# First pair of row blocks by halves with eight products a step, chunks loaded ahead of x, and operands of x built two blocks at a time

## The chip, the core and the metric

The kernel runs on one core of a Trainium2 chip. The metric is the device time of one execution in microseconds (us); less is better. Engines: TensorE (PE, with its weight loads as PEld), VectorE (DVE), ScalarE (ACT), GpSimd (POOL), and SyncE (SP), which here only issues loads. Each engine takes its instructions in the order of the program.

## What is computed

Everything is float32; N is 4096 rows, D is 512 columns, `adj` is 4096 x 4096.

```python
def reference(x, adj, L1_gnn_W):
    # layer 0
    mask = adj > 0
    head = mask / max(sqrt(sum(mask * mask, axis=-1)), 1e-12)
    inc = adj + head
    y = (inc @ x) / sum(inc, axis=-1)
    x = layernorm(x + y)
    # layer 1
    A2 = adj + eye
    dscale = diagonal(A2) ** -0.5
    temp = A2 @ x @ W.T
    x = layernorm(x + relu((dscale[:, None] * A2 * dscale[None, :]) @ temp))
    return x
```

(This is the reference in short; names are shortened.)

## The kernel before

Rows and columns of the large matrices are halved, and a product of 2 x 2 blocks is made of seven products of sums of blocks (S1 to S4 from the left operand, T1 to T4 from the right one) instead of eight. Layer 0 is the part that the change touches. It works on 16 *pairs* j: row blocks j and j + 16 of 128 rows each. The inner dimension of a pair is 16 *steps* kk (blocks kk and kk + 16 of x), taken in four *chunks* of four steps. One chunk of `adj` is a tile `a` of 128 partitions x 4 quarters x 512 (1 MB), with the quarters in the order A12, A11, A22, A21: the first two belong to the upper row block, the last two to the lower. A step is seven products with a 128 x 128 left operand and 256 columns (258 with the ones column that gives the row sums), accumulated in seven PSUM banks over the 16 steps (`multiply1`, L417).

The order of the work is written by hand: the program order is the order on every engine. Around a chunk it is: load the chunk after next (`load_chunk`, on SP's queue), prepare the next chunk (`prepare1`, on DVE), multiply this one (`multiply1`), count signs for a later pair (`count`, on ACT).

`prepare1` per chunk: raw sums A11 + A21 and A22 + A21 for layer 1 (L383), stored by POOL's queue (`oa`, L403); for each half the mask (`adj > 0`) times the row's scale (L393) and its addition to `a` (L395); then S1 to S4 (`add_up`, L159 to L162). On the main diagonal the identity goes into the raw sums (L166).

The scale of a row is one over the root of its number of positive entries. Since the rows lie on the free axis of a chunk, the scale has to stand in every partition. For pairs 1 to 15, ACT counts signs in tiles of `adj` in its natural layout (`nat`, 128 x 512, five buffers, loaded on SP's queue, L302 and L336), 16 tiles a pair; `spread` then sums, takes the root and the reciprocal, puts it on a diagonal `d`, and a product with ones spreads it over the partitions (L368), copied to `sc` (L370). For pair 0 it is counted from the chunks themselves (`count_first`): ACT makes bfloat16 signs of each whole chunk, 32 products with ones sum them up (L320), and DVE and ACT take root and reciprocal of 256 values (L306 to L323). This needs all four chunks of pair 0, so the fourth is loaded into an extra tile (`last`), and once more later as a chunk.

A block of x has a slot `b` of seven operands: B11, B21, B22 (raw quarters of x), T1, T2, T3 and T4; the fourth raw quarter, B12, is loaded in the place of T4. `build` makes T1 to T4 with four DVE operations of 128 x 256 (L123 to L126). The slots stay for the whole of layer 0.

At the start SP's queue holds: x of steps 0 to 3 (two loads of 256 KB each, L289 and L290), three chunks and `last` (1 MB each), then x of steps 4 to 15 with five `nat` loads among them. DVE builds the first four slots, then waits for the scale, prepares chunk 0 in four pieces of one step each, and in pair 0 builds the four slots of the next chunk ahead of each `prepare1` (L494 to L496). At the end of a pair, `combine` puts the seven banks together into the upper and lower row block; `layer0` normalises them and `operands` stores them for layer 1 in the course of the next pair.

Of the kernel before, what the change touches and what calls it, by code (L numbers as in the profile page):

```python
# [8 lines left out]
F32 = mybir.dt.float32  # L9
# [17 lines left out]
def tile_adj_resnorm_d2(  # L27
# [79 lines left out]
    nc.gpsimd.memset(tiny, -(2.0 ** -63))  # L107
    dscale = const.tile([P, NB], F32, name="dscale")
# [12 lines left out]
    def outer_sums(t, b11, b12, b21, b22):  # L121

        nc.vector.tensor_sub(t[:, 0, :], b11, b12)  # L123
        nc.vector.tensor_sub(t[:, 2, :], b22, b12)
        nc.vector.scalar_tensor_tensor(t[:, 1, :], t[:, 0, :], -1.0, b22, op0=ALU.mult, op1=ALU.subtract)
        nc.vector.tensor_add(t[:, 3, :], b21, t[:, 1, :])  # L126
# [142 lines left out]

    ones_f = w1_pool.tile([P, P], F32, name="ones_f", bufs=1)  # L270
    nc.gpsimd.memset(ones_f, 1.0)
    ones_b = w1_pool.tile([P, P], BF16, name="ones_b", bufs=1)
    nc.gpsimd.memset(ones_b, 1.0)
# [3 lines left out]
    def half_tile(dtype=F32, width=CW):  # L277
        return w1_pool.tile([P, 2, width], dtype, tag="u", name="u", bufs=3)
# [6 lines left out]
    def load_x(kk):  # L285

        s = feats_pool.tile([P, 7, W], F32, name=f"b{kk}")
        lo, hi = x[kk * P:(kk + 1) * P, :], x[(kk + NP) * P:(kk + NP + 1) * P, :]
        nc.sync.dma_start(out=s[:, B11:T4 + 1:T4, 0:H], in_=split(lo))  # L289
        nc.sync.dma_start(out=s[:, B21:B22 + 1, 0:H], in_=split(hi))  # L290
        nc.gpsimd.memset(s[:, B11:B21 + 1, H:W], 1.0)
        nc.gpsimd.memset(s[:, T1, H:W], 1.0)
        slots[kk] = s

    def build(kk):

        s = slots[kk]
        outer_sums(s[:, T1:T4 + 1, 0:H], s[:, B11, 0:H], s[:, T4, 0:H], s[:, B21, 0:H], s[:, B22, 0:H])
# [5 lines left out]
    def to_scale(n, total):  # L304

        nc.vector.tensor_scalar(n, total, 0.5, N / 2, op0=ALU.mult, op1=ALU.add)  # L306
        nc.vector.tensor_scalar(n, n, EPS * EPS, None, op0=ALU.max)
        nc.scalar.activation(n, n, AF.Sqrt)

    def count_first(parts):  # L310

        ps = spare()[:, 0:2 * P].rearrange("p (h i) -> p h i", h=2)
        for c, a in enumerate(parts):
            m = half_tile(BF16, 2 * CW)
            m = m.rearrange("p h (q i) -> p (h q) i", q=2)
            signs(m, a)
            for i in range(CK):
                for z in range(2):
                    first, last = c + i + z == 0, c == NC - 1 and i == CK - 1 and z == 1
                    nc.tensor.matmul(ps, ones_b, m[:, z::2, i * P:(i + 1) * P], start=first, stop=last)  # L320
        s = w1_pool.tile([P, 2, P], F32, name="sc")
        to_scale(s, ps)
        nc.vector.reciprocal(s, s)  # L323
        scale[0] = s
# [24 lines left out]
    spreading = {}  # L349

    def spread(j, part):

        if part == 0:
# [3 lines left out]
            spreading[j] = n  # L357
        elif part == 1:
            n = spreading.pop(j)
            nc.vector.reciprocal(n, n)  # L360
            d = w1_pool.tile([P, 2, P], F32, name="d", bufs=1)
            for h in range(2):
                nc.vector.tensor_scalar(d[:, h, :], ident, n[:, h:h + 1], None, op0=ALU.mult)
            spreading[j] = d
        else:
            d = spreading.pop(j)
            ps = spare()
            nc.tensor.matmul(ps[:, 0:2 * P], ones_f, d.rearrange("p h i -> p (h i)"), start=True, stop=True)  # L368
            s = w1_pool.tile([P, 2, P], F32, name="sc")
            nc.scalar.copy(s.rearrange("p h i -> p (h i)"), ps[:, 0:2 * P])  # L370
            scale[j] = s

    def prepare1(n, pieces=1):


        j, c = divmod(n, NC)
        a, s = chunks[n], scale[j]
        sr, *masks = (half_tile() for _ in range(3))
        sums[n] = work.tile([P, 4, CW], F32, tag="s", name="s")
        for i in range(pieces):  # L380
            w = CW // pieces
            cols = slice(i * w, (i + 1) * w)
            nc.vector.tensor_add(sr[:, :, cols], a[:, A11:A22 + 1, cols],  # L383
                                 a[:, A21, cols].unsqueeze(1).to_broadcast([P, 2, w]))
            for h in range(2):
                t = masks[h]
                y, z = t[:, :, cols], a[:, 2 * h:2 * h + 2, cols]
                if pieces == 1:
                    parts = [[v.rearrange("p q (b i) -> p (q b) i", i=P) for v in (y, z)]]
                else:  # L390
                    parts = [[v[:, q, :].rearrange("p (b i) -> p b i", i=P) for v in (y, z)] for q in range(2)]
                for m, v in parts:
                    nc.vector.scalar_tensor_tensor(m, v, 0.0, s[:, h, :].unsqueeze(1).to_broadcast(list(v.shape)),  # L393
                                                   op0=ALU.is_gt, op1=ALU.mult)
                nc.vector.tensor_add(a[:, 2 * h:2 * h + 2, cols], a[:, 2 * h:2 * h + 2, cols], t[:, :, cols])  # L395
            add_up(sums[n][:, :, cols], a[:, :, cols])
# [8 lines left out]
    def multiply1(n, acc):  # L405
        c = n % NC
        a, s = chunks.pop(n), sums.pop(n)
        for i in range(CK):
            kk = c * CK + i
            b = slots[kk]  # L410
            cols = slice(i * P, (i + 1) * P)
            for m, (left, right, w) in enumerate((
# [4 lines left out]
                nc.tensor.matmul(acc[m][:, 0:w], left, b[:, right, 0:w], start=(kk == 0), stop=(kk == NP - 1))  # L417

# [49 lines left out]
    for kk in range(CK):  # L468
        load_x(kk)
    for n in range(3):  # L470
        load_chunk(n)
    last = work.tile([P, 4, CW], F32, tag="s", name="s")
    nc.sync.dma_start(out=last, in_=adj_q[0, NC - 1])
    for kk in range(CK, NP):
        load_x(kk)
        if kk >= 2 * CK and len(waiting) < 5:
            load_natural()
    for kk in range(CK):
        build(kk)
    count_first([chunks[0], chunks[1], chunks[2], last])  # L480
    prepare1(0, pieces=CK)

    C = None
    for n in range(NP * NC):
        j, c = divmod(n, NC)
        if c == 0:
            if j > 0:
                C = combine(acc)
            acc = [bank(m) for m in range(7)]
        if n + 2 >= NP * NC:  # L490
            load_up_to(n + 2 - NP * NC)
        elif n > 0:
            load_chunk(n + 2)
        if j == 0 and c < NC - 1:  # L494
            for kk in range((c + 1) * CK, (c + 2) * CK):
                build(kk)  # L496
        if j + 1 < NP and c == (3 if j == 0 else 2):
            spread(j + 1, 0)
            if j == 0:
                spread(1, 1)  # L500
                spread(1, 2)
        if n + 1 < NP * NC:
            prepare1(n + 1)
        else:
            prepare(0)
        if 0 < j < NP - 1 and c == 2:
            spread(j + 1, 1)
        multiply1(n, acc)
        if 0 < j < NP - 1 and c == 2:
            spread(j + 1, 2)  # L510
        count(((5, 5, 6, 4) if j == 0 else (6, 6, 0, 4))[c])
# [4 lines left out]
        if j > 0 and c == 1:  # L516
            layer0(j - 1, C)
        if j > 0 and c == 2:
# [294 lines left out]
```

## Time and profile before

| | us |
|---|---|
| median of 3 runs | 2346.43 (2346.09 to 2346.45) |
| the profiled execution | 2345.41 |
| its span, first to last instruction | 2343.6 |
| TensorE busy in the span | 2277.4 (97%) |
| DVE busy | 1832.7 (78%) |
| ACT busy | 351.5 (15%) |
| mean granted TensorE clock | 0.990 of full |

All durations come from the profiled execution, which lasted 1.0 us less than the median of the runs. "Busy" is the time in which an engine worked on an instruction; weight loads are counted apart and lie beside the products. Line numbers (L417) are lines of the kernel before. In the chain of waits each piece is the work that held up what follows it; the page leaves out pieces too short to matter. An arrow such as `a<-adj_q` says which tile was written from which tensor. A float32 product on TensorE leaves two records in the trace.

### The profile page before, as it was taken

To read this page: it belongs to the slowest core of one execution; us is meant where nothing else is said; L and a number is where in the kernel's file an instruction comes from. 1 tells how busy PE (TensorE), PEld (TensorE's weight loads), DVE (VectorE), ACT (ScalarE), POOL (GpSimd) and SP (SyncE) were. 2 spreads that over 40 slices of the span, in tenths; PEclk is the share of its full clock that TensorE was granted. 3 is DMA by queue.
4 is the path that set the end of the run, shared out by engine and by line. 5 is a ranking of instruction groups with operands and counts; after the bars stand their busy time and mean duration, and the time that the engine had idled before them with its cause. 6 is when DMAs were issued, how large, how long until landed. Compare 5 with 4: busy or idle time off the path is not lost.

```text
span 2343.6 us, 21028 instructions
## 1 busy us (share of the span) xinstructions
PE 2277.4 (97%) x7166; PEld 1352.6 (58%) x7166; DVE 1832.7 (78%) x2727; ACT 351.5 (15%) x806; POOL 220.7 (9%) x372
## 2 busy tenths in 40 slices
PE   4999999999999999999999999999999999999996
PEld 3788888888888844444444444444444444444443
DVE  6898888888889857888666779766567798767796
ACT  3232333323333000000000000000000011200013
POOL 0011111111111110000001100011100000000010
PEclk8999999999999999999999999999999999999998
DMA  9577777777776466575566757567666576765672
GB/s 318 197 252 252 262 244 253 258 255 260 251 256 235 172 261 242 207 276 204 202 252 229 274 186 267 186 237 286 225 238 223 214 253 237 267 231 216 224 260 77
DMA packets 148011, 552.97 MB, mean 236 GB/s; under 512 B 15920, under 2 KB 24128, under 8 KB 108864
## 3 DMA queue, kind: packets, MB, share of 16 engines
q1 hardware_dynamic: 114192, 418.42, 51.0%
q0 software_dynamic: 33712, 133.21, 14.9%
q8 instruction: 57, 0.93, 0.2%
q14 instruction: 50, 0.41, 0.0%
HBM read 438.32 MB, written 113.25 MB: 235 GB/s over the span
## 4 chain that ended last, share of the span: by engine, by line
PE 86%; DVE 8%; issue 3%; DMA 2%; ACT 0%; POOL 0%; SPq 0%; ACTq 0%; DVEq 0%; POOLq 0%
PE q L252 55%; PE q L417 26%; PE q L625 5%; DVE a L395 1%; DVE u L393 1%; DVE s L159 1%; DMA a<-oa 1%; DVE u L383 1%; DMA s<-adj_q 1%; DVE s L161 1%; PE q L645 1%; DMA oa<-u 0%; DVE c L553 0%; DVE s L162 0%; PE q L368 0%
## 5 line engine op out<-in xcount | busy, mean ns | idle before, releaser
L252 PE MATMUL q<-s,ts 128*128 128x512 f32 x1344 | 616.0, 594 | 1.0 <-DVE u L544 1.0
L417 PE MATMUL q<-b,s 128*128 128x256 f32 (+1 forms) x2048 | 488.5, 381 | 2.3 <-DVE s L161 2.3
L159 DVE TENSOR_TENSOR s<-a 128x1024 f32<-128x1024 f32 (+1 forms) x243 | 294.1, 1210 | 203.5 <-PE q L252 173.8
L252 PEld LDWEIGHTS q<-s,ts 128*128 128x128 f32 x1344 | 256.2, 191 | 325.7 <-issue 296.6
L417 PEld LDWEIGHTS q<-b,s 128*128 128x128 f32 x2048 | 389.8, 190 | 61.0 <-DVE s L161 3.7
L417 PE MATMUL q<-b,a 128*128 128x258 f32 (+1 forms) x1536 | 381.8, 383 | 10.1 <-issue 10.1
L252 PE MATMUL q<-a,tr 128*128 128x512 f32 x704 | 333.5, 596 | 5.1 <-DMA tr<-ob 4.2
L417 PEld LDWEIGHTS q<-b,a 128*128 128x128 f32 x1536 | 293.9, 192 | 52.9 <-issue 10.7
L252 PE MATMUL q<-s,tr 128*128 128x512 f32 x448 | 228.8, 592 | 0.0
L252 PEld LDWEIGHTS q<-a,tr 128*128 128x128 f32 x704 | 132.1, 191 | 162.1 <-issue 158.1
L302 ACT ACTIVATE nat<-nat,tiny 128x512 f32<-128x512 f32 x240 | 171.0, 715 | 208.2 <-DMA nat<-adj 208.1
L252 PE MATMUL q<-a,ts 128*128 128x512 f32 x352 | 180.2, 593 | 3.1 <-DVE c L549 2.9
L393 DVE SCALAR_TENSOR_TENSOR u<-a,sc 128x1024 f32<-128x1024 f32 (+1 forms) x142 | 157.6, 1114 | 24.8 <-ACT sc L370 14.4
L161 DVE TENSOR_TENSOR s<-a,s 128x512 f32<-128x512 f32 (+1 forms) x243 | 166.5, 685 | 8.3
L162 DVE TENSOR_TENSOR s<-a,s 128x512 f32<-128x512 f32 (+1 forms) x243 | 166.5, 685 | 8.3
L395 DVE TENSOR_TENSOR a<-a,u 128x1024 f32<-128x1024 f32 (+1 forms) x134 | 157.7, 1177 | 6.8
L252 PEld LDWEIGHTS q<-s,tr 128*128 128x128 f32 x448 | 85.1, 190 | 107.3 <-issue 99.0
L542 ACT COPY p<-q 128x512 f32<-128x512 f32 x28 | 16.4, 585 | 754.9 <-PE q L252 754.9
L252 PEld LDWEIGHTS q<-a,ts 128*128 128x128 f32 x352 | 66.5, 190 | 88.7 <-issue 77.0
L625 PE MATMUL q<-wt,c 128*128 128x512 f32 x256 | 115.1, 592 | 0.0
L159 DVE TENSOR_TENSOR s<-r 128x1024 f32<-128x1024 f32 x48 | 58.7, 1223 | 70.1 <-PE q L252 65.0
L403 POOL DMA_DIRECT2D oa<-u x64 | 57.6, 901 | 465.8 <-DVE u L383 211.2
(121 smaller groups left out, 1581.2 us busy)
## 6 DMA issues: line engine op xcount, KB each, us to landing
a<-adj_r SPq DMA_DIRECT2D x112, 1024.0 KB, 6.1
a<-oa SPq DMA_DIRECT2D x80, 1024.0 KB, 5.3
a<-adj_q SPq DMA_DIRECT2D x64, 1024.0 KB, 6.1
nat<-adj SPq DMA_DIRECT2D x240, 256.0 KB, 6.9
tr<-ob SPq DMA_DIRECT2D x112, 512.0 KB, 3.7
oa<-u POOLq DMA_DIRECT2D x64, 512.0 KB, 7.9
oa<-r POOLq DMA_DIRECT2D x32, 1024.0 KB, 6.6
y<-x POOLq DMA_DIRECT2D x64, 256.0 KB, 6.1
```

The lines of the kernel that those rows point to most:

```text
L159: nc.vector.tensor_add(s[:, S3:S1 + 1, :], a[:, A11:A22 + 1, :], a[:, A21, :].unsqueeze(1).to_broadcast([P, 2, w]))
L161: nc.vector.tensor_add(s[:, S2, :], a[:, A11, :], s[:, S1, :])
L162: nc.vector.tensor_add(s[:, S4, :], a[:, A12, :], s[:, S2, :])
L252: nc.tensor.matmul(acc[m], left, right, start=(kk == 0), stop=(kk == NQ - 1))
L302: nc.scalar.activation(y, a, AF.Sign, bias=tiny, scale=2.0 ** 64, accum_out=accum)
L383: nc.vector.tensor_add(sr[:, :, cols], a[:, A11:A22 + 1, cols], a[:, A21, cols].unsqueeze(1).to_broadcast([P, 2, w]))
L393: nc.vector.scalar_tensor_tensor(m, v, 0.0, s[:, h, :].unsqueeze(1).to_broadcast(list(v.shape)), op0=ALU.is_gt, op1=ALU.mult)
L395: nc.vector.tensor_add(a[:, 2 * h:2 * h + 2, cols], a[:, 2 * h:2 * h + 2, cols], t[:, :, cols])
L403: nc.gpsimd.dma_start(out=dst, in_=sr.rearrange("p m (k i) -> p (m k) i", i=P))
L417: nc.tensor.matmul(acc[m][:, 0:w], left, b[:, right, 0:w], start=(kk == 0), stop=(kk == NP - 1))
L625: nc.tensor.matmul(pv, C_of[2][h][f][:, 2 * r + e, cols], wt[:, 2 * f + e, :], start=(f + e == 0), stop=(f + e == 2))
L645: nc.tensor.transpose(ps[:, at + i * P:at + (i + 1) * P], C_of[3][h][d // 2][:, 2 * r + d % 2, cols], ident)
```

## The change

Pair 0 is taken out of the loop and written out. Its upper row block is computed first, as four plain products a step with raw quarters of x into two banks (`multiply_plain(0, c)`), then its lower row block in the same way: eight products a step in all, no S sums and no T sums. The chunks of pair 0 are loaded by halves: the four upper halves ahead of everything, then x of steps 0 to 9, the four lower halves, and x of steps 10 to 15. All four are kept, the fourth in a tile of `work`; nothing is loaded twice. Signs are counted for each half by itself (`count_half`, `scale_half`), for the lower one in the middle of the upper half's products. A11 with its mask goes into a tile of its own (`inc11`), since the raw sums still need the raw A11. The row blocks are copied out of PSUM by ACT (`take`) instead of `combine`.

`build` now takes two blocks (a slot is half of a tile `feats[g]`) with two operations, and `build_last` makes T4 later, after the plain products with the raw quarter in its place. In later pairs `prepare1` is put together from `raw_sums` and `to_inc`, with one mask tile in the place of two; `spread` takes its second and third part earlier. An early square root on ACT comes first of all. The count of tiles is the same (16 + 4 in pair 0).

```diff
+    half_n = const.tile([P, 1], F32, name="half_n")
+    nc.gpsimd.memset(half_n, N / 2)
+
+    nc.scalar.activation(small.tile([P, 1], F32, name="sd"), eps_t, AF.Sqrt)
...
-        s = feats_pool.tile([P, 7, W], F32, name=f"b{kk}")
...
         nc.sync.dma_start(out=s[:, B11:T4 + 1:T4, 0:H], in_=split(lo))
         nc.sync.dma_start(out=s[:, B21:B22 + 1, 0:H], in_=split(hi))
-        nc.gpsimd.memset(s[:, B11:B21 + 1, H:W], 1.0)
-        nc.gpsimd.memset(s[:, T1, H:W], 1.0)
-        slots[kk] = s
-
-    def build(kk):
-
-        s = slots[kk]
-        outer_sums(s[:, T1:T4 + 1, 0:H], s[:, B11, 0:H], s[:, T4, 0:H], s[:, B21, 0:H], s[:, B22, 0:H])
+
+    def build(g):
+
+        s = feats[g][:, :, :, 0:H]
+        nc.vector.tensor_sub(s[:, :, T1:T3 + 1:2, :], s[:, :, B11:B22 + 1:2, :],
+                             s[:, :, T4:T4 + 1, :].to_broadcast([P, 2, 2, H]))
+        nc.vector.scalar_tensor_tensor(s[:, :, T2, :], s[:, :, T1, :], -1.0, s[:, :, B22, :], op0=ALU.mult, op1=ALU.subtract)
+
+    def build_last(g):
+
+        s = feats[g][:, :, :, 0:H]
+        nc.vector.tensor_add(s[:, :, T4, :], s[:, :, B21, :], s[:, :, T2, :])
...
-        nc.vector.tensor_scalar(n, total, 0.5, N / 2, op0=ALU.mult, op1=ALU.add)
-        nc.vector.tensor_scalar(n, n, EPS * EPS, None, op0=ALU.max)
-        nc.scalar.activation(n, n, AF.Sqrt)
...
-    def count_first(parts):
-
...
-            signs(m, a)
...
-        s = w1_pool.tile([P, 2, P], F32, name="sc")
-        to_scale(s, ps)
-        nc.vector.reciprocal(s, s)
-        scale[0] = s
+        nc.scalar.activation(n, total, AF.Sqrt, bias=half_n, scale=0.5)
+
+    def count_half(h, c, ps):
+
+        m = w1_pool.tile([P, 2, CW], F32, name="sr", bufs=2).bitcast(BF16)[:, :, 0:CW]
+        signs(m, chunks[c][:, 2 * h:2 * h + 2, :])
+        for z in range(2):
+            nc.tensor.matmul(ps, ones_b, m[:, z, :], start=(c + z == 0), stop=(c == NC - 1 and z == 1))
+
+    def scale_half(h, ps):
+        n = scale[0][:, h, :]
+        nc.vector.tensor_reduce(n, ps.rearrange("p (b i) -> p i b", i=P), axis=mybir.AxisListType.X, op=ALU.add)
+        to_scale(n, n)
+        nc.vector.tensor_scalar(n, n, EPS, None, op0=ALU.max)
+        nc.vector.reciprocal(n, n)
...
             to_scale(n, n)
-            spreading[j] = n
+            scale[j] = n
         elif part == 1:
-            n = spreading.pop(j)
+            n = scale.pop(j)
+            nc.vector.tensor_scalar(n, n, EPS, None, op0=ALU.max)
             nc.vector.reciprocal(n, n)
             d = w1_pool.tile([P, 2, P], F32, name="d", bufs=1)
             for h in range(2):
                 nc.vector.tensor_scalar(d[:, h, :], ident, n[:, h:h + 1], None, op0=ALU.mult)
-            spreading[j] = d
+            scale[j] = d
...
-            nc.scalar.copy(s.rearrange("p h i -> p (h i)"), ps[:, 0:2 * P])
...
-    def prepare1(n, pieces=1):
...
+            scale[j] = w1_pool.tile([P, 2, P], F32, name="sc")
+            nc.scalar.copy(scale[j].rearrange("p h i -> p (h i)"), ps[:, 0:2 * P])
+
+    def raw_sums(n):
...
         j, c = divmod(n, NC)
-        a, s = chunks[n], scale[j]
-        sr, *masks = (half_tile() for _ in range(3))
-        sums[n] = work.tile([P, 4, CW], F32, tag="s", name="s")
-        for i in range(pieces):
-            w = CW // pieces
-            cols = slice(i * w, (i + 1) * w)
-            nc.vector.tensor_add(sr[:, :, cols], a[:, A11:A22 + 1, cols],
-                                 a[:, A21, cols].unsqueeze(1).to_broadcast([P, 2, w]))
...
-                nc.vector.tensor_add(a[:, 2 * h:2 * h + 2, cols], a[:, 2 * h:2 * h + 2, cols], t[:, :, cols])
-            add_up(sums[n][:, :, cols], a[:, :, cols])
+        a, sr = chunks[n], w1_pool.tile([P, 2, CW], F32, name="sr", bufs=2)
+        nc.vector.tensor_add(sr, a[:, A11:A22 + 1, :], a[:, A21, :].unsqueeze(1).to_broadcast([P, 2, CW]))
         if j // CK == c:
             add_identity(sr[:, :, (j % CK) * P:(j % CK + 1) * P])
...
+    def masks(n, h, cols):
+
+        y, z, s = mask[:, :, cols], chunks[n][:, 2 * h:2 * h + 2, cols], scale[n // NC][:, h, :]
+        if cols == slice(0, CW):
+            parts = [[v.rearrange("p q (b i) -> p (q b) i", i=P) for v in (y, z)]]
+        else:
+            parts = [[v[:, q, :].rearrange("p (b i) -> p b i", i=P) for v in (y, z)] for q in range(2)]
+        for m, v in parts:
+            nc.vector.scalar_tensor_tensor(m, v, 0.0, s.unsqueeze(1).to_broadcast(list(v.shape)),
+                                           op0=ALU.is_gt, op1=ALU.mult)
+        return y, z
+
+    def to_inc(n, h):
+
+        y, z = masks(n, h, slice(0, CW))
+        nc.vector.tensor_add(z, z, y)
+
+    def upper_inc(c, cols):
+
+        y, z = masks(c, 0, cols)
+        nc.vector.tensor_add(inc11[:, c, cols], z[:, A11, :], y[:, A11, :])
+        nc.vector.tensor_add(z[:, A12, :], z[:, A12, :], y[:, A12, :])
...
+    def prepare1(n, between=None):
+        if n not in early:
+            raw_sums(n)
+        if between is not None:
+            between()
+        sums[n] = work.tile([P, 4, CW], F32, tag="s", name="s")
+        for h in range(2):
+            to_inc(n, h)
+        add_up(sums[n], chunks[n])
+
+    def multiply1(n, acc, then=None):
         c = n % NC
         a, s = chunks.pop(n), sums.pop(n)
         for i in range(CK):
             kk = c * CK + i
             b = slots[kk]
             cols = slice(i * P, (i + 1) * P)
+            if then is not None and i == CK - 1:
...
+    def multiply_plain(h, c, acc, then=None):
+
+        a = chunks[c]
+        for i in range(CK):
+            kk = c * CK + i
+            cols = slice(i * P, (i + 1) * P)
+            if then is not None and i == 1:
+                then()
+            k1, k2 = (a[:, A21, cols], a[:, A22, cols]) if h else (inc11[:, c, cols], a[:, A12, cols])
+            for left, ops in ((k1, (B11, T4)), (k2, (B21, B22))):
+                for y, op, w in zip(acc, ops, (W, H)):
+                    nc.tensor.matmul(y[:, 0:w], left, slots[kk][:, op, 0:w], start=(kk == 0 and left is k1),
+                                     stop=(kk == NP - 1 and left is k2))
+
+    def take(h, acc):
+
+        y = row_tile("z", 4)
+        nc.scalar.copy(y[:, 0:H], acc[0][:, 0:H])
+        nc.scalar.copy(y[:, H:D], acc[1][:, 0:H])
+        nc.scalar.copy(deg0[:, h:h + 1], acc[0][:, H:H + 1])
+        return y
...
+    feats = [feats_pool.tile([P, 2, 7, W], F32, name=f"b{g}") for g in range(NP // 2)]
+    for kk in range(NP):
+        slots[kk] = feats[kk // 2][:, kk % 2]
+    for n in range(NC):
+        chunks[n] = ring.tile([P, 4, CW], F32, tag="a", name="a") if n < NC - 1 else \
+            work.tile([P, 4, CW], F32, tag="s", name="s")
+    inc11 = work.tile([P, 4, CW], F32, tag="s", name="s")
+    scale[0] = w1_pool.tile([P, 2, P], F32, name="sc")
+    deg0 = small.tile([P, 2], F32, name="deg")
+
...
+    for c in range(NC):
+        load_half(0, c)
+    ps = spare()
+    for c in range(NC):
+        count_half(0, c, ps)
+    for kk in range(10):
         load_x(kk)
-    for n in range(3):
-        load_chunk(n)
-    last = work.tile([P, 4, CW], F32, tag="s", name="s")
-    nc.sync.dma_start(out=last, in_=adj_q[0, NC - 1])
-    for kk in range(CK, NP):
+    for c in range(NC):
+        load_half(1, c)
+    for kk in range(10, NP):
         load_x(kk)
-        if kk >= 2 * CK and len(waiting) < 5:
-            load_natural()
-    for kk in range(CK):
-        build(kk)
-    count_first([chunks[0], chunks[1], chunks[2], last])
-    prepare1(0, pieces=CK)
-
-    C = None
...
+    for s in feats:
+        nc.gpsimd.memset(s[:, :, B11:B21 + 1, H:W], 1.0)
+        nc.gpsimd.memset(s[:, :, T1, H:W], 1.0)
+    for _ in range(5):
+        load_natural()
+    top, low = [bank(0), bank(1)], [bank(6), bank(5)]
+    scale_half(0, ps)
+    upper_inc(0, slice(0, P))
+    upper_inc(0, slice(P, CW))
+    upper_inc(1, slice(0, CW))
+    multiply_plain(0, 0, top)
+    build(0)
+    upper_inc(2, slice(0, CW))
+    multiply_plain(0, 1, top)
+    build(1)
+    build(2)
+    upper_inc(3, slice(0, CW))
+    ps = spare()
+    multiply_plain(0, 2, top, lambda: [count_half(1, c, ps) for c in range(NC)])
+    build(3)
+    scale_half(1, ps)
+    count(16)
+    build(4)
+    raw_sums(0)
+    to_inc(0, 1)
+    multiply_plain(0, 3, top)
+    top = take(0, top)
+    build(5)
+    raw_sums(1)
+    to_inc(1, 1)
+    multiply_plain(1, 0, low)
+    load_chunk(NC)
+    spread(1, 0)
+    build(6)
+    build_last(0)
+    raw_sums(2)
+    to_inc(2, 1)
+    spread(1, 1)
+    build_last(1)
+    multiply_plain(1, 1, low)
+    load_chunk(NC + 1)
+    spread(1, 2)
+    count(4)
+    raw_sums(3)
+    to_inc(3, 1)
+    build_last(2)
+    build(7)
+    early = {NC}
+    raw_sums(NC)
+    multiply_plain(1, 2, low)
+    build_last(3)
+    prepare1(NC)
+    build_last(4)
+    multiply_plain(1, 3, low)
+    C = top, take(1, low), deg0
+    load_rows(0)
+
+    for n in range(NC, NP * NC):
         j, c = divmod(n, NC)
         if c == 0:
-            if j > 0:
+            if j > 1:
...
-        elif n > 0:
+        else:
             load_chunk(n + 2)
-        if j == 0 and c < NC - 1:
-            for kk in range((c + 1) * CK, (c + 2) * CK):
-                build(kk)
-        if j + 1 < NP and c == (3 if j == 0 else 2):
+        scales = j < NP - 1 and c == 2
+        if scales:
             spread(j + 1, 0)
...
         if n + 1 < NP * NC:
-            prepare1(n + 1)
+            prepare1(n + 1, between=(lambda: spread(j + 1, 1)) if scales else None)
         else:
             prepare(0)
-        if 0 < j < NP - 1 and c == 2:
-            spread(j + 1, 1)
-        multiply1(n, acc)
-        if 0 < j < NP - 1 and c == 2:
-            spread(j + 1, 2)
-        count(((5, 5, 6, 4) if j == 0 else (6, 6, 0, 4))[c])
+        if n == NC:
+            for g in range(5, NP // 2):
+                build_last(g)
+        multiply1(n, acc, (lambda: spread(j + 1, 2)) if scales else None)
+        count((6, 6, 0, 4)[c])
...
-        if j > 0 and c == 1:
+        if c == 1:
             layer0(j - 1, C)
-        if j > 0 and c == 2:
+        elif c == 2:
```

`load_half(h, c)` loads quarters 2h and 2h + 1 of chunk c on SP's queue.

## The prediction, made before the result was known

> **What bounds the kernel now.** I read the page's chain of work that ended last first, then the busy time of each engine in stretches of 20 us, then the chain and the timeline of the first 140 us.
>
> ```profile
> PE 86%; DVE 8%; issue 3%; DMA 2%; ACT 0%; POOL 0%; SPq 0%; ACTq 0%; DVEq 0%; POOLq 0%
> ...
> 0.00:20.00 20.00, 3.23 (x15) 2.20 (x16) 6.00 (x16) 6.59 (x4) 2.94 (x43) 1.00 0.88 325
> 20.00:40.00 20.00, 14.48 (x60) 11.49 (x59) 14.92 (x45) 8.26 (x14) 0.00 (x0) 0.83 1.08 367
> 40.00:60.00 20.00, 11.90 (x40) 9.11 (x39) 19.56 (x40) 7.82 (x20) 1.80 (x2) 0.74 0.70 241
> 60.00:80.00 20.00, 19.75 (x91) 16.62 (x89) 19.48 (x30) 0.81 (x2) 1.77 (x2) 1.00 0.51 184
> 80.00:100.00 20.00, 14.98 (x61) 12.84 (x62) 15.03 (x25) 5.31 (x15) 1.99 (x3) 0.83 0.47 158
> 100.00:120.00 20.00, 20.00 (x94) 17.49 (x93) 18.21 (x21) 7.35 (x21) 1.80 (x2) 1.00 0.84 290
> ```
>
> The window columns are length, PE, weight loads, DVE, ACT, POOL, PE clock, DMA share, GB/s. TensorE is the bound of the whole, but in the first 100 us it starves: only from 100 us on is it full. From 26.8 to 85 us the chain runs through DVE:
>
> ```profile
> 8.06 12.58 DMA s<-adj_q
> 20.75 2.01 ACT u L302
> 22.80 1.05 PE q L320 x8
> 25.11 1.75 DVE sc L323
> ...
> 85.02 1.22 PE q L368 x2
> 86.24 49.88 PE q L417 x224
> ```
>
> Full signs wait for the fourth whole chunk (landed 20.64); the first product starts at 28.07. Per later chunk of pair 0, DVE needs 8.5 us of preparation (1.14 + 2 x 1.15 + 2 x 1.23 + 1.24 + 0.70 + 0.69) and 5.8 us of building four blocks, against 12.1 us of products. A product has two records: 33.59 us for 155 of them after 136.55 us gives 0.433 us each. The piece from 86.24 holds the last 28 products of pair 0 and 84 of pair 1 and ends at 136.12, so pair 0's products end at 136.12 - 84 x 0.433 = 99.7 us, and SP agrees: it issues the load that this end frees at 99.75. Call it E; all later work hangs on TensorE from there, so the change is worth E(before) - E(after).
>
> **What the Trainium skill says.** "TensorE: Matmul & The Clock Gate", part 1: an idle matmul array falls to half its clock and needs about 3.4 us of sustained work to return. The trace agrees roughly: the granted clock is 0.50 from 27.6 to 34.2, from 47 to 58 and from 82 to 88.7 us, each time after a pause. "DMA: Bandwidth & Descriptors", on the anatomy of a DMA: some 2 us fixed, then 436 GB/s. Here chunks move at 414 to 438 GB/s between 12 and 18 us, and x (1 KB pieces) at 233 to 289 at the start and 350 to 375 mixed with others. "ScalarE: Activation LUTs", what a table load costs: 1283 ns plus a drain of 1380. The trace shows 1283 ns at 13.40 and the activation right after it, so no drain.
>
> **The change, part by part.**
>
> Loads. SP now issues four upper half chunks (2.1 MB) first, then ten blocks of x (5.2 MB), four lower halves (2.1 MB), six blocks of x (3.1 MB), five count tiles. The total is unchanged, so the bytes moved in before give the times: cumulated windows reach 9.4 MB at 28.1 us and 12.6 MB at 36.5; landings lag the moved bytes by 1.4 us (the chunk that landed at 13.34 was 3.15 MB, 3.72 were moved). SP keeps eight DMAs in flight (its issue at 20.66 waits for the one eight before), which covers that lag. Upper halves: 2.2 + 2.1 MB at 390 GB/s + 1.4 = 9.0 us. At 240 GB/s, as x had, it is 12.4; at 430, 8.5. Lower halves 29.5, last x 37.9.
>
> Start. ACT's sign of 1,024 elements is half of L302's 1.99 us: 1.05. The table is loaded ahead by the new early square root; both loads of before were under waits, so it is worth nothing. Then two 512-wide bf16 products (cold, 0.43 each by L320's 0.2 per 256), a reduction of 512 PSUM elements (not in the trace; 0.70 by L141's 695 ns over 512, bounds 0.5 to 1.0), square root 0.6 with its gaps, max 0.25, reciprocal 0.95 (half of 1.75), and the first quarter of the upper masks, 1.2 (25.11 + 1.75 to 28.07 is the like). 9.0 + 1.05 + 0.86 + 0.7 + 0.6 + 0.25 + 0.95 + 1.2 + 0.4 of gaps = 15.0 us, 13 us sooner than 28.07.
>
> Products. 8 instead of 7 a step: 128 x 0.433 = 55.4 us, 6.9 more. The upper 64 take raw x: no build and only 2.4 us of DVE a chunk (1.15 + 2 x 0.69) against 6.9 us of products, so DVE no longer holds them. Cold clock: 2.5 us (between 0, if the counting keeps it warm, and 3.4). TensorE reaches the end of block 8 at 15.0 + 2.5 + 15.6 = 33.1; lower halves (29.5) and x (block 15 needed at 46.8, there at 37.9) are in time.
>
> The count of the lower halves is queued on TensorE there. Its sign tiles have two buffers, so signs 3 and 4 wait for the products of 1 and 2: two products 0.43, sign 1.05, sign 1.05, two products 0.43, gaps: 3.3 us on the path (1.7 if none waited, 5 if the halves are late). Behind it all products wait. Then 7 blocks end the upper half at 33.1 + 3.3 + 12.1 = 48.5. The two lower quarters need 2.4 us of DVE a chunk, plus 1.15 for the raw sums: DVE has the first at 36.4 + 2.8 (scale) + 1.9 (build) + 1.5 + 2.4 = 45.0. In time. Lower half: 27.7 plus 0.43 for pair 1's scale: E = 76.6. What is left of pair 0's sums S1 to S4 is nothing: 2.65 us a chunk gone from DVE.
>
> Builds. One pair is 1.22 (1,024 elements, as L159) + 0.65 + 0.69 = 2.6 us against 2 x 1.44: 2.2 us off DVE over eight pairs, hidden under products. T4 is built late, since the raw quarter in its place is read until the lower pass is done with it: DVE waits behind TensorE, but reaches each late build several us after those products.
>
> The second path. DVE's reduction for pair 1's scale stands behind 16 count tiles on ACT, and everything for the lower chunks 2 and 3 and for pair 1 stands behind it on DVE. The tiles follow x: 12.6 + 4.2 MB and part of 1 MB of stores at 375 GB/s put the last at about 52, its sign ends at D = 53 (0.75 us a tile; ACT alone would take 0.71). DVE then needs 7.2 us to the scale's diagonal (D + 7.2 = 60.2; TensorE wants it at 62.4) and 22.5 us to pair 1's S2: 0.2 + builds of 2.6, raw sums and masks 3.5, diagonal 0.9, late build 0.7, 3.5, 2.6, raw 1.1, late 0.7, masks 4.8, 1.94 (75.5; wanted at E + 0.9 = 77.5). Two us of slack: this is what comes next.
>
> SP. Pair 1's first chunk is queued behind those count tiles and waits for lower chunk 0's products (55.5); it lands about 61, used from 67. POOL only stores the raw sums. Stores take 7.9 us, and two buffers turn over in 9 or more.
>
> Later pairs. Diagonal and broadcast of the scale move some us ahead. One wait of 0.5 us shows between 150 and 770 us in the waits (PE L368 on DVE d); it goes. Combining pair 0 (3.3 us of DVE at 97.7) becomes ACT copies.
>
> Sum: 99.7 - 76.6 + 0.5 = 23.6 us. The profiled execution took 2345.41 (span 2343.6), the median of the runs is 2346.43; I take the same difference from it: 2322.8.
>
> **Rivals.**
> A, the forecast: TensorE is the bound from 15 us on. For it: the windows above. With the start between 13 and 17.5, clock 0 to 3.4, count 1.7 to 5, it holds 2319 to 2326.
> B: count tiles bound. Issue to landing took 6.4 us in the first 60 us; over five buffers, with sign, 1.2 to 1.4 us a tile. The first tile lands at about 39.5, so D = 39.5 + 16 x 1.3 = 60.3, and pair 1 starts 0.9 us before its S2: E = D + 22.5 - 0.9 = 82: 2328.5. Against it: much of that 6.4 was queueing behind x.
> C: masks wait for whole chunks, as the lower half loads into the same tile: first mask at 29.5, E = 30.7 + 61.6 = 92.3: 2338.5. Against it: in before DVE starts on a block at 3.87, between its two loads.
> D, slower: the same count loop, if a tile takes over 2.4 us: D = 78, E = 99.7. At 3 us D = 87.5, E = 109: 2355.7. In its favour: signs came every 2.1 us between 28.7 and 37.1. Against it: two loads of x stood between them.
>
> **How the numbers follow.** A 0.60, B 0.22, C 0.07, earlier than A's range 0.05, D 0.04, about even 0.02. A, B and the earlier start give 2318.0 to 2331.0, worth 0.85. Changes below 0.2% (4.7 us) can't be told from none here. Faster 0.94, same 0.02, slower 0.04.
>
> **What would show it.** Right: first product near 15, a gap near 33 of under 4 us, pair 0 ending near 77, no gap on TensorE before pair 1. Wrong: DVE idle over 5 us before pair 1's count reduction, or the first product after 20.

## The result and the profile after

| | us |
|---|---|
| before, median of 4 runs | 2346.44 (2346.09 to 2347.89) |
| changed, median of 4 runs | 2325.91 (2325.34 to 2326.94) |
| ratio | 0.9912, 95% interval 0.9895 to 0.9929 |
| its profiled execution and span | 2326.30, 2324.4 |
| forecast | 2322.8, range 2318.0 to 2331.0 |

The change took 20.5 us off; 23.6 were forecast. First the page of the changed kernel, its chain of waits by engine:

```profile
PE 93%; DVE 4%; DMA 2%; issue 1%; ACT 0%; SPq 0%; ACTq 0%; DVEq 0%
```

Then its busy time in the same 20 us stretches as before (length, PE, weight loads, DVE, ACT, POOL, clock, DMA share, GB/s):

```profile
0.00:20.00 20.00, 8.34 (x18) 4.46 (x19) 6.94 (x14) 6.48 (x7) 2.44 (x28) 1.00 0.96 304
20.00:40.00 20.00, 18.70 (x83) 15.16 (x83) 14.30 (x18) 4.89 (x5) 0.00 (x0) 1.00 1.07 368
40.00:60.00 20.00, 20.00 (x94) 17.51 (x93) 13.18 (x16) 13.05 (x36) 1.80 (x2) 1.00 0.85 282
60.00:80.00 20.00, 18.60 (x87) 15.99 (x86) 19.62 (x25) 3.85 (x12) 3.76 (x5) 1.00 0.91 314
80.00:100.00 20.00, 19.82 (x92) 17.05 (x91) 19.48 (x20) 9.27 (x26) 1.80 (x2) 1.00 0.66 217
```

TensorE is full from 20 us on but for two holes, the count between 33 and 38 us and 1.4 us near 64 (20.00 - 18.60), and 0.2 us near 80.7. In the kernel before it lacked 5.5 of 20 us between 20 and 40, 8.1 between 40 and 60 and 5.0 between 80 and 100. DVE's share of the whole chain fell from 8% to 4%. The start of the changed kernel's chain (pieces left out are marked, the last piece ends at 113.5 us):

```profile
2.12 7.85 DMA s<-adj_q
...
10.07 1.16 ACT sr L312
...
11.27 1.01 PE q L323 x2
12.29 3.43 issue
15.71 18.66 PE q L450 x72
34.38 0.45 PE q L323 x2
...
35.95 1.14 ACT sr L312
...
37.14 0.59 PE q L323 x2
37.73 26.03 PE q L450 x120
...
79.99 0.70 DVE s L168
...
80.74 32.76 PE q L437 x150
```

L312 makes signs, L323 counts, L450 are the plain products, L437 the seven-product steps of pair 1. The last upper half has landed at 9.97 us, against 20.64 for the fourth chunk before; the first product starts at 15.71. ("Issue" of 3.43 us is the time in which DVE and ACT make the scale and DVE the first masks; the chain names no releaser for it.) Its waits, TensorE and DVE, from 15 to 90 us:

```profile
PE q L450 <- issue: 3.4, 1, 3.4
PE q L373 <- DVE d L368: 1.4, 1, 1.4
PE q L323 <- ACT sr L312: 1.3, 2, 0.9
PE q L437 <- DVE s L168: 0.2, 1, 0.2
...
DVE n L359 <- ACT nat L312: 6.5, 1, 6.5
DVE sc L327 <- PE q L323: 5.0, 1, 5.0
```

L373 is the broadcast of pair 1's scale, L359 the reduction of its counts. Two waits were not in the forecast: 1.4 us of L373 for the diagonal `d`, and 0.2 us for S2. Both hang on DVE's 6.5 us behind the count tiles.

### The profile page after: what moved, and what is told of

It reads as the page before. It is cut to its first block, busy times and chain, and to the rows that moved or that the text cites. A ratio compares the mean times of both kernels' runs of the same rounds, so it can differ in the third digit from the quotient of the medians.

```text
span 2324.4 us, 21026 instructions
## 1 busy us (share of the span) xinstructions
PE 2278.8 (98%) x7182; PEld 1355.4 (58%) x7182; DVE 1817.9 (78%) x2631; ACT 353.7 (15%) x815; POOL 220.3 (9%) x357
## 3 DMA queue, kind: packets, MB, share of 16 engines
q0 software_dynamic: 33712, 133.21, 15.6%
## 4 chain that ended last, share of the span: by engine, by line
PE 93%; DVE 4%; DMA 2%; issue 1%; ACT 0%; SPq 0%; ACTq 0%; DVEq 0%
PE q L259 54%; PE q L437 31%; PE q L726 5%; PE q L450 2%; DMA a<-oa 1%; DVE s L166 1%; PE q L746 1%; DMA a<-adj_r 0%; DVE c L654 0%; DMA s<-adj_q 0%; DVE s L168 0%; PE q L373 0%; DMA a<-adj_q 0%; DVE c L658 0%; DVE r L232 0%
## 5 line engine op out<-in xcount | busy, mean ns | idle before, releaser
L437 PE MATMUL q<-b,s 128*128 128x256 f32 (+1 forms) x1920 | 454.4, 379 | 0.2 <-DVE s L168 0.2
L166 DVE TENSOR_TENSOR s<-a 128x1024 f32<-128x1024 f32 x236 | 288.8, 1224 | 207.5 <-PE q L259 169.5
L437 PEld LDWEIGHTS q<-b,s 128*128 128x128 f32 x1920 | 363.8, 190 | 52.6 <-DVE s L168 0.6
L437 PE MATMUL q<-b,a 128*128 128x258 f32 (+1 forms) x1440 | 354.0, 380 | 0.0
L437 PEld LDWEIGHTS q<-b,a 128*128 128x128 f32 x1440 | 273.3, 190 | 38.5
L312 ACT ACTIVATE nat<-nat,tiny 128x512 f32<-128x512 f32 x240 | 171.0, 715 | 181.4 <-DMA nat<-adj 180.6
L168 DVE TENSOR_TENSOR s<-a,s 128x512 f32<-128x512 f32 x236 | 163.3, 692 | 8.1
L169 DVE TENSOR_TENSOR s<-a,s 128x512 f32<-128x512 f32 x236 | 163.3, 692 | 8.0
L398 DVE SCALAR_TENSOR_TENSOR mask<-a,sc 128x1024 f32<-128x1024 f32 (+2 forms) x129 | 154.2, 1197 | 2.1
L405 DVE TENSOR_TENSOR a<-a,mask 128x1024 f32<-128x1024 f32 x123 | 150.7, 1225 | 6.6 <-DVE mask L398 0.5
L388 POOL DMA_DIRECT2D oa<-sr x64 | 57.7, 901 | 390.2 <-DVE sr L381 250.8
```

What stands on the lines that cost most here:

```text
L166: nc.vector.tensor_add(s[:, S3:S1 + 1, :], a[:, A11:A22 + 1, :], a[:, A21, :].unsqueeze(1).to_broadcast([P, 2, w]))
L168: nc.vector.tensor_add(s[:, S2, :], a[:, A11, :], s[:, S1, :])
L169: nc.vector.tensor_add(s[:, S4, :], a[:, A12, :], s[:, S2, :])
L312: nc.scalar.activation(y, a, AF.Sign, bias=tiny, scale=2.0 ** 64, accum_out=accum)
L388: nc.gpsimd.dma_start(out=dst, in_=sr.rearrange("p m (k i) -> p (m k) i", i=P))
L398: nc.vector.scalar_tensor_tensor(m, v, 0.0, s.unsqueeze(1).to_broadcast(list(v.shape)), op0=ALU.is_gt, op1=ALU.mult)
```

## Experiments

All marks are starts in the profiled execution, in us: first product; count of the lower halves on TensorE (end of step 8); next product; end of the sixteenth sign of count tiles; pair 1's first product, the E of the forecast. At full clock steps 0 to 8 take 36 x 0.433 = 15.6 us. "vs before" is the ratio to the kernel before on the same chip, with its interval.

| run | first | count | next | sign 16 | pair 1 | vs before |
|---|---|---|---|---|---|---|
| before | 28.10 | | | 74.07 | 99.7 | 1 |
| changed | 15.71 | 34.22 | 37.57 | 57.80 | 79.52 | 0.9912 (0.9895 to 0.9929) |
| after_again | 15.58 | 33.66 | 37.01 | 57.49 | 79.21 | 0.9911 (0.9896 to 0.9926) |
| late_scale | 15.68 | 33.49 | 36.84 | 57.03 | 77.16 | 0.9907 (0.9892 to 0.9922) |
| warm | 23.00 | 41.11 | 44.46 | 61.68 | 84.78 | 0.9942 (0.9927 to 0.9956) |
| late_and_warm | 23.09 | 40.78 | 44.13 | 59.95 | 84.45 | 0.9934 (0.9917 to 0.9950) |
| nat4 | 15.62 | 33.23 | 36.58 | 59.30 | 82.70 | 0.9924, a single run |
| nat6 | 15.64 | 34.27 | 37.62 | 55.21 | 77.94 | 0.9908 (0.9893 to 0.9922) |
| late_signs | 15.53 | 32.95 | 34.68 | 58.49 | 75.00 | 0.9900 (0.9885 to 0.9915) |
| late_warm | 15.44 | 31.12 | 34.47 | 58.49 | 74.84 | 0.9898 (0.9883 to 0.9913) |
| all_three | 15.64 | 31.32 | 33.55 | 57.94 | 74.29 | 0.9892 (0.9875 to 0.9908) |
| x_first | 22.70 | 39.93 | 43.28 | 59.97 | 83.60 | 0.9936 (0.9921 to 0.9951) |
| single_builds | 15.83 | 33.58 | 36.93 | 57.13 | 78.96 | 0.9920 (0.9903 to 0.9938) |
| before_chunks_first | 24.90 | | | 70.17 | 97.7 | 0.9985 (0.9978 to 0.9992) |

late_scale, warm, late_and_warm and nat4 ran on one chip, after_again, late_signs, late_warm and all_three on a second, the other four on a third; the kernel before took 2349.42, 2347.44 and 2347.68 us there, so times that an expectation names are to be read against 2346.44. The marks tell kernels apart better than the totals do. Layer 1 is the same code in all; from the end of layer 0 on, the profiled executions took 1509.0 us (the kernel before) to 1515.9 us. A difference of 2 us in a total can come from there; whether that spread is chance or follows from layer 0 in some way wasn't tried.

Theory: pair 0 has two paths of nearly the same length, TensorE's own and the one from the count tiles on ACT through DVE to `d` and S2. Rival: TensorE alone, and the forecast only had the start and the clock a little wrong.

### The second path taken out of the way

```diff
-    spread(1, 0)
     build(6)
     build_last(0)
     raw_sums(2)
     to_inc(2, 1)
-    spread(1, 1)
     build_last(1)
     multiply_plain(1, 1, low)
     load_chunk(NC + 1)
-    spread(1, 2)
-    count(4)
     raw_sums(3)
     to_inc(3, 1)
+    spread(1, 0)
     build_last(2)
     build(7)
+    spread(1, 1)
     early = {NC}
     raw_sums(NC)
-    multiply_plain(1, 2, low)
+    multiply_plain(1, 2, low, lambda: spread(1, 2))
+    count(4)
```

> The changed kernel with DVE's reduction for pair 1's scale (and what follows from it) moved behind the masks of lower chunks 2 and 3, and the broadcast product moved behind the first step of lower chunk 2. Two-path theory: DVE no longer sits idle 6.5 us behind the count tiles, the 1.40 us wait of TensorE for the diagonal d goes, and the wait of 0.2 us for S2: pair 1's first product at 78.1 instead of 79.5, time 1.5 us below the changed kernel (2324.4). Rival (the 2.7 us between my 76.6 and the measured 79.5 come only from a later start, a colder clock and slower products): TensorE stays at 79.5 and the time at 2325.9.

Pair 1 started at 77.16. Of the 2.36 us, 0.7 come from a shorter half-clock stretch in that execution (steps 0 to 8 took 17.81 instead of 18.51), the rest, 1.6, from the wait for `d` with what is lost around it. The wait for S2 comes after pair 1's first product and so after this mark. In its waits of TensorE from 15 to 90 us both are gone:

```profile
PE q L450 <- issue: 3.4, 1, 3.4
PE q L323 <- ACT sr L312: 1.3, 2, 0.9
```

So the rival isn't the whole cause. The totals don't tell: 0.9907 against 0.9912, with intervals that overlap. DVE now waits 2.4 us for pair 1's first chunk instead: SP reaches that load at 58.4, behind the count tiles, and it takes 8 us to land. S2 is ready at 75.7, and TensorE doesn't see it.

### Count tiles: buffers or bandwidth

```diff
-        nat = w1_pool.tile([P, NAT], F32, tag="nat", name="nat", bufs=5)
+        nat = w1_pool.tile([P, NAT], F32, tag="nat", name="nat", bufs=4)
...
-    for _ in range(5):
+    for _ in range(4):
         load_natural()
```

(With 6 in the same places for nat6.)

> The changed kernel with four instead of five buffers for the count tiles. If the pace of the count tiles (1.06 us each) is set by the turn of a buffer (sign, issue, load of about 4 us), eleven tiles take 5/4 as long: last sign at 57.8 + 3 = 60.8, DVE's diagonal 3 us later, TensorE waits 4.4 us for it, pair 1 at 82.5. If the pace is set by what the DMA engines can move, nothing changes: 57.8 and 79.5.

> The changed kernel with six buffers for the count tiles. With four the sixteenth sign ended at 59.3, with five at 57.5 to 57.8. If a buffer's turn sets the pace it ends at 56 to 56.3, the wait for d (1.4 to 1.6) goes and pair 1 starts at 78.0 to 78.4. If the DMA engines set it: 57.5 and 79.2 to 79.5.

The sixteenth sign ended at 59.3, 57.8 and 55.2 with four, five and six buffers: 1.15, 1.06 and 0.91 us a tile from the first sign (40.93, 40.77, 40.70). TensorE's wait for `d` was 3.9, 1.4 and 0 us, the first two by these lines of the waits (nat4, then nat6):

```profile
PE q L373 <- DVE d L368: 3.9, 1, 3.9
...
DVE n L359 <- ACT nat L312: 9.0, 1, 9.0
```

```profile
DVE n L359 <- ACT nat L312: 3.9, 1, 3.9
```

So buffers set the pace in good part, though a fifth one brought 1.5 us and not 3; the sixth brought 2.3 to 2.6. The DMA columns of the changed kernel (last two: share, GB/s) show why it is a mixture:

```profile
40.00:44.00 4.00, 4.00 (x20) 3.51 (x19) 3.86 (x6) 3.23 (x9) 0.08 (x1) 1.00 0.64 206
44.00:48.00 4.00, 4.00 (x21) 3.49 (x20) 3.93 (x5) 2.04 (x6) 0.83 (x1) 1.00 0.83 255
48.00:52.00 4.00, 4.00 (x20) 3.51 (x19) 3.36 (x3) 2.78 (x7) 0.89 (x1) 1.00 0.98 333
52.00:56.00 4.00, 4.00 (x21) 3.48 (x20) 0.00 (x0) 2.43 (x7) 0.00 (x0) 1.00 0.99 359
```

From 40 to 48 us the DMA engines are only 64 to 83% busy, though tiles are still to be loaded: a load waits until ACT has freed a buffer. ACT signs the first five tiles back to back (40.77 to 44.3) and then waits 0.4 and 1.7 us for the seventh and eighth (45.71 and 48.24). From 48 on they are full, with 512 KB of raw sums among the tiles. DVE (third busy column) does nothing at all from 52 to 56. The four-buffer run also lost 1.7 us to half clock after its pause of 3.9 us: the 32 plain products after it, which take 13.9 us at full clock, took 15.6. Its mark of 82.70 lies next to the expected 82.5 by luck: the tiles cost 1.5 us less than expected, and the half clock was not in the sum.

### A warm clock at the first product

```diff
         count_half(0, c, ps)
+        for _ in range({1: 10, 3: 32}.get(c, 0)):
+            nc.tensor.matmul(bank(2)[:, 0:P], ones_b, ones_b, start=True, stop=True)
```

> The changed kernel with 42 small products of ones in a bank not yet in use, 10 after the second and 32 after the fourth upper count, so that TensorE works while the scale is made; they add nothing to the result. The clock should be full at the first product or 1 to 2 us after, which takes up to 2.5 us of the 3.1 us of half clock away. Two-path theory: the diagonal of pair 1's scale still comes at 65, since it hangs on the count tiles, so TensorE only waits longer for it (about 4 us instead of 1.4) and pair 1 starts at 79.5 as before: time 2325.9 within 0.5. Rival (TensorE is the only path): pair 1 starts at 77, time 2323.4.

> Both edits. Two-path theory: the two gains, of which the second alone is worth nothing, add up when the other path is out of the way: pair 1 starts at 75.5 to 76, time 2321.5 to 2322.5. Rival that the late scale alone gives nothing and the warm clock all: same as warm alone, 2323.4.

Neither tested what it should. In the code each of these products takes a new tile of the same bank, and I read their pace, 0.32 us a piece, as a wait for the one before; the profile names no releaser for it. The first real product came at 23.0 (the timeline of warm):

```profile
12.93 10.23 PE L529 MATMUL q<-ones_b 128*128 128x128 bf16 x32
23.00 2.05 PE L450 MATMUL q<-b,s 128*128 128x258 f32 x4
```

The clock was still at half (two products in 2.05 us): these 42 products in 13 us didn't raise it. The run still tells something: TensorE began 7.3 us later and pair 1 only 5.3 us. With the wait for `d` and what is lost around it (1.6 us) gone and 0.4 us less of half clock, 7.3 - 2.0 = 5.3: the two-path sum, from the other side.

The second attempt, on top of the late scale:

```diff
+        again = {1: 3, 3: 8}.get(c, 0) if h == 0 else 0
+        w = bank(2) if again else None
+        for i in range(again):
+            nc.tensor.matmul(w, ones_b, m[:, 0, :], start=(i == 0), stop=(i == again - 1))
```

> The late scale with 11 products of ones and signs, 512 wide, in one unused bank as one accumulation each (3 after the second upper count, 8 after the fourth), so that they follow each other without the wait for the bank that made the 42 of the run warm take 0.32 us each. They add nothing to the result. First product at 15.7 to 16; of the 2.2 us of half clock in late_scale 1 to 2.2 go: pair 1 at 75 to 76.2. If the clock needs something else than this work to rise, 77.2.

Its chain of waits:

```profile
12.01 1.73 PE q L327 x8
13.74 1.70 issue
15.44 15.85 PE q L454 x72
31.29 0.45 PE q L323 x2
```

The eight extra products ran at 0.22 us each, so the clock rose on the way, and it held through 1.7 us of pause: 36 products in 15.85 us instead of 18.66. Pair 1 started at 74.84, 2.3 us before late_scale: 2.1 of it in steps 0 to 8, 0.2 at the first product. Half clock at the start cost up to 3 us and can be had back. Which of the two differences from warm did it, longer products or one accumulation without a new tile each, wasn't tried apart.

### The count of the lower halves

```diff
-        m = w1_pool.tile([P, 2, CW], F32, name="sr", bufs=2).bitcast(BF16)[:, :, 0:CW]
+        if h and c > 1:
+            m = mask.bitcast(BF16)[:, :, (c - 2) * CW:(c - 1) * CW]
+        else:
+            m = w1_pool.tile([P, 2, CW], F32, name="sr", bufs=2).bitcast(BF16)[:, :, 0:CW]
```

> The late scale of before, and the third and fourth sign tile of the lower count put into the mask tile, so that these signs don't wait for products on TensorE. If the 3.2 us from block 8 to block 9 are eight products of 0.22 us and two signs in between, they fall to 1.75 us and pair 1 starts at 75.7 instead of 77.2 (S2 is ready at 75.7 there, wanted 0.9 after the start, so it doesn't hold it). If the lower halves themselves were late, the gap stays at 3.2.

> Late scale, signs in the mask tile and the warming products. TensorE alone would give 73.5 to 74.7. Then DVE comes next: pair 1's first chunk can't be loaded before lower chunk 0 is done with its buffer, lands 8 us later and needs 9.2 us of DVE to S2. TensorE is done with chunk 0 about 3 us sooner, but SP stands behind the count tiles until 58.4, so S2 stays near 75.7 and holds the third product of pair 1 for up to 1.5 us: a gain of 2.5 us over late_scale at most, 24 to 25 us below the kernel before.

late_signs, chain of waits:

```profile
15.53 17.58 PE q L453 x72
33.11 1.73 PE q L326 x8
34.84 1.30 PE q L453 x6
```

The gap is 1.73 us instead of 3.35, as worked out: it was the two sign buffers, not late halves. Pair 1 came 2.2 us before late_scale's: 1.6 from the count, 0.4 from a shorter stretch of half clock, 0.15 from the start. All three edits together start pair 1 at 74.29, 0.6 to 0.7 us before either pair of them; TensorE alone would have given about 73. I had expected S2 to hold its third product, and it did not: S2 was ready at 74.6, wanted at 75.2. The count, needed sooner, had to wait for the last sign (2.2 us of gap instead of 1.7; ACT could begin the third sign only at 30.87, when DVE was done with the mask tile), and `d` cost 0.18 us, by these waits of TensorE:

```profile
PE q L326 <- ACT mask L312: 0.3, 1, 0.3
PE q L380 <- DVE d L375: 0.2, 1, 0.2
```

The total was 2323.26 us beside 2326.90 of the changed kernel on the same chip and 2347.44 of the kernel before. The three together thus beat both kernels by the medians; against the changed kernel the intervals overlap, and the 4.9 us between their marks (79.21 to 74.29) are the firmer figure.

### Parts of the change by themselves

```diff
+    for kk in range(CK):
+        load_x(kk)
     for c in range(NC):
         load_half(0, c)
...
-    for kk in range(10):
+    for kk in range(CK, 10):
         load_x(kk)
```

> The changed kernel with the first four blocks of x loaded ahead of the upper halves again: this part of the change undone. The last upper half lands at 15.8 instead of 10.0 (in the kernel before, 4.2 MB of x and chunks had landed at 15.78), so the first product moves from 15.7 to 21.5; the 1.4 us wait for the diagonal d goes, since TensorE is later there: pair 1 at 79.5 + 5.8 - 1.4 = 83.9, time 4.4 us above the changed kernel. Rival (the loads' order alone made most of the gain of 20): 90 or later.

```diff
-    for kk in range(CK):
-        load_x(kk)
     for n in range(3):
         load_chunk(n)
     last = work.tile([P, 4, CW], F32, tag="s", name="s")
     nc.sync.dma_start(out=last, in_=adj_q[0, NC - 1])
+    for kk in range(CK):
+        load_x(kk)
```

> The kernel before with its four chunks loaded ahead of x: the loads' part of the change alone. The chunks land at 13.4 and their count is done at 16.5, but DVE first builds four blocks of x, which land at 19.5: first product at 25 instead of 28.1. From there DVE bounds pair 0 as before, so pair 1 starts 3 us sooner, at 96.7, time 3 us below the kernel before. Rival (loads' order makes the gain): first product near 18 and 8 to 12 us below.

The loads' order is worth 7 us at the first product in the changed kernel (1.2 more than I had expected), 4.1 to 4.4 at pair 1 and about 6 by the ratios (0.9936 - 0.9911, each within 0.0015). The 4.1 are 7.0 less the 1.6 us around the wait for `d`, which is gone, and 1.3 us less of half clock in that execution. Alone, in the kernel before, it is worth 3.2 us at the first product, 2.0 at pair 1 and 3.0 by the medians (2347.68 to 2344.65). Its first product, at 24.9, waits for four builds of x, as its chain shows; the first block of x lands at 15.0, and DVE goes from there through four builds to the scale:

```profile
3.66 11.35 DMA b<-x
15.04 0.43 DVE b L124
15.47 0.34 DVE b L125
...
20.34 0.42 DVE b L126
20.77 0.34 DVE sc L306
...
21.91 1.75 DVE sc L323
```

So 16 of the 20 us at pair 1 (99.7 to 83.6, in x_first) don't come from the loads' order. The marks and the price of a product say where the 20.2 us are. TensorE starts 12.4 us sooner and has 6.9 us more of products. What is left of pair 0 beside products and broadcast, holes and half clock, fell from 22.7 us (99.7 - 28.1 - 48.5 - 0.4) to 8.0 (79.5 - 15.7 - 55.4 - 0.4): 12.4 + 14.7 - 6.9 = 20.2. Builds by twos are worth half a us, as the next run shows. That the rest belongs to the plain products by halves, which need no build and little preparation, so that DVE no longer stands in front of every chunk, is argued from what is left over and not shown by a run: plain products without the halves weren't tried, nor the smaller parts of the change (one mask tile, the earlier `spread`, copies by ACT) by themselves.

```diff
-        s = feats[g][:, :, :, 0:H]
-        nc.vector.tensor_sub(s[:, :, T1:T3 + 1:2, :], s[:, :, B11:B22 + 1:2, :],
-                             s[:, :, T4:T4 + 1, :].to_broadcast([P, 2, 2, H]))
+        for b in range(2):
+            s = feats[g][:, b, :, 0:H]
+            nc.vector.tensor_sub(s[:, T1, :], s[:, B11, :], s[:, T4, :])
+            nc.vector.tensor_sub(s[:, T3, :], s[:, B22, :], s[:, T4, :])
```

(T2 and T4 likewise.)

> The changed kernel with x's operands built one block at a time (three operations and a late one each of 128 x 256): this part undone. A pair takes 2.9 us of DVE instead of 2.6. Where DVE has slack it costs nothing; behind the count tiles it has none, and there two builds and four late builds add 0.4 us up to the diagonal and 1.1 us up to S2: pair 1 starts at 79.9 and its third product waits another 1 us; time 1 to 1.5 us above the changed kernel. If DVE were not on the path, 0.

Pair 1 started at 78.96, since the sixteenth sign came 0.4 to 0.7 us sooner here; from that sign to `d`'s broadcast it was 7.45 us instead of 7.34, and the wait for S2 grew from 0.2 to 0.5 us. By these marks the expectation of 1 to 1.5 us was two to three times too high: building by twos is worth about half a us here. The totals, 0.9920 against 0.9911 (2 us), have intervals that overlap and can't decide.

## Why the prediction was near, and where it was off

The forecast named the mechanism: TensorE bounds pair 0 from its first product on, and E moves from 99.7 to 76.6. E is 79.5, halfway between the forecast and rival B (82). The stated range took in both, so that the result lies inside it doesn't choose between them; the steps do.

| step of the forecast | forecast | measured |
|---|---|---|
| last upper half landed | 9.0 | 9.97 |
| first product | 15.0 | 15.7 |
| half clock in steps 0 to 8 | 2.5 | 2.9 |
| end of step 8 | 33.1 | 34.2 |
| count on the path | 3.3 | 3.35 |
| end of upper half | 48.5 | 49.7 |
| D, last sign of the count tiles | 53 | 57.8 |
| TensorE can broadcast `d` | D + 7.2 | D + 7.3 |
| S2 ready | D + 22.5 | D + 22.9 |
| pair 1 | 76.6 | 79.5 |

**Right.** The start (the last upper half landed 1.0 us late, and the chain of small steps behind it was 0.3 us shorter than its sum), the count with its wait for two buffers (its cause shown by late_signs), eight products at 0.433 us with x and lower halves in time, DVE's sum to `d` and to S2 and the order in which they come next. The 0.5 us wait of a later pair is gone: TensorE waits for `d` nowhere after pair 0. Rival C (masks wait for whole chunks) is excluded by the first product at 15.7.

**Off.** The largest part of the miss is one mis-sized term: the pace of the count tiles, put at 0.75 us from what the DMA engines can move; it was 1.06. D came 4.8 us later. That used up the 2.2 us of slack on DVE's path and the 1.2 us by which TensorE itself was late, and put 1.4 us of waiting on TensorE, where the forecast had named no gap. Rival B had in good part the right mechanism, five buffers, and too high a pace (1.3). The sign that I had named for being wrong, DVE idle over 5 us before pair 1's reduction, was there: 6.5 us. The other parts of the 2.9 us: 0.7 at the start, 0.4 of half clock, 0.1 at the count, 0.2 around the wait (from 49.71 to the first product behind the broadcast it was 15.9 us, 14.3 without a wait, and the wait itself is 1.4). Chunk 4, expected at 61, was issued only at 58.8, behind the count tiles; in the changed kernel it was used at 71.5 and cost nothing.

**The rest.** Layer 0 ended at 814.0 instead of 834.6, 20.6 us sooner. Layer 1 then took 1510.4 us against 1509.0 in the two profiled executions, within what untouched code varied by. The prediction's 2 us of fixed cost of a DMA stands in its page for DMAs that GpSimd issues; the loads here are SP's, and the sum used the measured lag of 1.4 us, so nothing hangs on it.

## What to carry to other kernels

Where the first stage starves for prepared operands, a dearer form of the product that takes raw operands can be the faster one: here it added 6.9 us of TensorE, and the whole change still brought 20 us, 4 of them by the order of the loads. When that is done, look for a second path of about the same length before crediting every edit: TensorE already waited 1.4 us for the path behind the count tiles, so by the same sum a warmer clock or a shorter count alone would only have lengthened that wait. Both were run only with that path out of the way. And a loop with a handful of buffers has a pace of its own; take the number of loads under way into the sum, not only the bytes.

## What the runs showed of the hardware

The granted-clock column read 1.00 from 0 to 40 us of the changed kernel, while its first products took 2.05 us for four records against 1.03 later: the first stretch of half clock shows only in the durations. "TensorE: Matmul & The Clock Gate" of the Trainium skill (part 1, on seeing it oneself) warns that the clock events of a trace shouldn't be fully trusted, and these agree. Its statement that the window in which activity is watched runs freely, so that the ramp varies, fits too, though no run here shows the window: with first products between 15.53 and 15.83 us the loss in steps 0 to 8 was 1.8 to 3.0 us over seven runs without extra products (17.42 to 18.63 - 15.6). At half clock a product takes twice its time, so these are stretches of about 3.6 to 6 us, longer than the 3.4 us that the prediction quotes.

A pause of 1.4 us (changed kernel) and one of 1.7 us (late_warm) left the clock full; after one of 3.9 us (nat4) the next 32 products lost 1.7 us to half clock.

The chain of waits named a release that held nothing: for the changed kernel it shows 5.28 us of `a<-adj_q` before 69.06, yet DVE, the next in the chain, worked 3.90 and 3.97 of 4 us between 64 and 72.
